# The last batch of a two-layer graph kernel: three side jobs moved earlier in the queues, and the last aggregation finished block by block

## The chip, the cores and the metric

The kernel runs on one core of a Trainium2 chip. The core has five engines with a queue each: TensorE (PE in the profile, with its weight loads as PEld), VectorE (DVE), ScalarE (ACT), GpSimd (POOL) and SyncE (SP), which here only issues DMAs. Each queue is worked off in the order in which the program emits its instructions, and an instruction at the head that waits for another engine holds up all that is queued behind it.

The metric is the time of one execution on the device, in microseconds, as the median of several runs. Before the change it is 2584.24 us, over three runs from 2582.49 to 2584.95 us.

## The reference

32 batches of 512 rows by 512 columns pass through two layers. Cut to what matters:

```
# layer 0: attention with 8 heads of 64, masked by adj, then a residual and a norm
q, k, v = x @ Wq + bq, x @ Wk + bk, x @ Wv + bv
scores  = q k^T / sqrt(64) + where(adj == 0, -1e9, 0)
x = layernorm(x + softmax(scores) v)
# layer 1: aggregation over the graph, a weight, a bias, a residual and a norm
y = adj @ x
x = layernorm(x + y @ weight + bias)
```

adj is a 512 by 512 matrix of zeros and ones, the same for all batches. The layer norm has no learned scale.

## The kernel before

A batch's rows are four blocks of 128 rows (the index c, r or row below), its columns four blocks of 128 columns (the index d). `X[b]` holds a batch's rows in SBUF. There is one tile for an even and one for an odd batch, and a separate one, `xlast`, for batch 31. The program is emitted in one long hand-made order: nothing reorders it, and it is this order that the change edits.

To keep float32 accuracy[...], the kernel splits each factor. For layer 1 the rows are split into a high half (ACT, `split` L503 or `split_rows` L537) and a low half (POOL, L504 or L538). **Aggregation** is y = adj @ x: eight matmuls for each block d of y, four with high halves and four with low halves. For batches 0 to 30 it is `aggregate` (L520), block by block: as soon as a block's eight matmuls are done, `split_y` (L514) splits it into three factors: high on ACT (`split_high`, L304), rest on DVE (`split_rest`, L307), both on POOL (`split_both`, L310). **Convolution** is y @ weight: `convolve` (L569) runs three passes of four matmuls for each row block into two PSUM banks, NEAR (high and rest factors) and FAR (both factors), so 48 matmuls for a batch and all eight banks. `add_row` (L578) then adds NEAR (L561) and FAR (L565) to `X[b]` on DVE, which also sets the banks free. The **bias** is added to `X[b]` on POOL (`add_bias`, L540). The **second norm** is: statistics of each row block on DVE (`statistics`, L477 and L478), one square root on ACT (L481), a reciprocal and four small products on DVE (`invert_root`, L486 and L488), one pass over each row block on ACT (`normalise`, L493); then `store` (L506) sends the batch out through SP. The tables for the norm are called by batch plus layer: `norm(t - 1, 1)` with t = 31 is batch 29's second norm, because layer 1 runs one batch behind, and `norm(t, 1)` is batch 30's. In the same way `norm(t, 0)` is batch 31's first norm.

In the main loop (`iteration`, L800) three batches are under way at once, and the side jobs of the older two are strewn among the matmuls of the youngest. The change leaves this loop alone. It edits what comes after it.

- `last_halves(31)` (L874): batch 31's attention; batch 29's last two row blocks are convolved and added; batch 30's rows are split (`splits`) and aggregated (`gathered`).
- The end (L959 on), with t = 31: batch 30 is convolved; batch 31's first norm, with `split_rows` after each normalised row block; batch 29's last statistics, second norm and store; batch 30's `add_row`s, last bias and statistics; batch 30's second norm; `aggregate_rows(31)` (L543); convolution of 31; `judge` (L713), five tiny DVE operations that say whether any value ran out of range; batch 30's store; and last, row block by row block, batch 31's adds, statistics, root, norm and store.

`aggregate_rows` has the row block c as its outer loop, so that it may begin when the first row block is normalised, and needs four banks at once. The banks are handed out in turn out of eight. Since the convolution of batch 30 just before took all eight, the aggregation waits until batch 30's first rows are added:

```
    run(survey(t - 2)[NB // 2:] + norm(t - 1, 1))
    store(t - 2)
    run([(add_row, t - 1, r) for r in range(NB)] + biases(t - 1)[3:] + survey(t - 1))
    run(biases(t)[:2] + norm(t, 1)[:2])
    aggregate_rows(t)
```

`survey(b)` is the four statistics of batch b, `biases(b)` its four bias additions, and `merge(a, b)` emits a[0], then all of b[0], then a[1], then all of b[1], and so on.

Of the kernel before, what the change touches and what calls it, by code (L numbers as in the profile page):

```python
# [18 lines left out]
P = 128  # L19
# [163 lines left out]
def fast_kernel(ctx: ExitStack, tc, verdict, x, adj, Wq, bq, Wk, bk, Wv, bv, W1, b1, out):  # L183
    nc = tc.nc
# [3 lines left out]
    NB = N // P  # L188
    DB = D // P
# [10 lines left out]
    def bank(*shape):  # L200

        return psum.tile([P, *shape], FP, name="bank", tag="bank", bufs=8)

    def plain(t):

        return t.bitcast(FP)
# [69 lines left out]
    adjT = work.tile([P, NB, N], FR, name="adjT", bufs=1)  # L276
# [26 lines left out]
    def split_high(high, a):  # L303
        nc.scalar.activation(high, a, AF.Copy, scale=EPSILON * SHRINK)  # L304

    def split_rest(rest, high, a):
        nc.vector.scalar_tensor_tensor(rest, plain(high), -1.0 / EPSILON, a, op0=ALU.mult, op1=ALU.add)  # L307

    def split_both(both, high, rest, engine=nc.gpsimd):
        engine.tensor_sub(both, plain(high), plain(rest))  # L310
# [16 lines left out]
    def factors():  # L327
        return [work.tile([P, DB, N], FR, name=f"factors{f}", bufs=1) for f in (HIGH, REST, BOTH)]
# [36 lines left out]
    def splits_of_x(b):  # L365
        return [[(f, b, d) for d in range(DB)] if b < B else [] for f in (high_of_x, rest_of_x, both_of_x)]
# [102 lines left out]
    STAT, RSTD, SHIFT, HIGHS, LOWS = {}, {}, {}, {}, {}  # L469
# [36 lines left out]
    def store(b, blocks=None):  # L506
        for c in blocks or ():
            nc.sync.dma_start(out[b, c * P:(c + 1) * P, :], X[b][:, c, :])
        if blocks is None:
            nc.sync.dma_start(out[b].rearrange("(c p) d -> p c d", p=P), X[b])  # L510

    YT = {}
# [27 lines left out]
    def add_bias(b, c):  # L540
        nc.gpsimd.tensor_add(X[b][:, c, :], X[b][:, c, :], b1_r)  # L541

    def aggregate_rows(b):  # L543

        banks = [bank(N) for _ in range(DB)]
        for c in range(NB):
            for d, pm in enumerate(banks):
                for part in (HIGHS[b, c], LOWS[b, c]):
                    nc.tensor.matmul(pm, part[:, d * P:(d + 1) * P], adjT[:, c, :],
                                     start=(c == 0 and part is HIGHS[b, c]), stop=(c == NB - 1 and part is LOWS[b, c]))  # L550
        YT[b] = factors()
        high, rest, both = ([YT[b][f][:, d, :] for d in range(DB)] for f in range(3))
        for d, pm in enumerate(banks):
            split_high(high[d], pm)
            split_rest(rest[d], high[d], pm)
        for d in range(DB):
            split_both(both[d], high[d], rest[d], nc.gpsimd if d < 2 else nc.vector)

    def add_near(b, r, near):
        row = X[b][:, r, :]  # L560
# [8 lines left out]
    def convolve(b, passes):  # L569

        yt = YT[b]
        for r, f, blocks in passes:
            if (b, r) not in NEAR:
                NEAR[b, r], FAR[b, r] = bank(N), bank(N)
            one_pass(f, (FAR if f == BOTH else NEAR)[b, r], lambda f, d: yt[f][:, d, r * P:(r + 1) * P],
                     lambda f, d: w1[:, f, d, :], blocks)
# [5 lines left out]
    def whole(r):  # L582
        return [(r, f, range(DB)) for f in (HIGH, REST, BOTH)]
# [5 lines left out]
    def aggregation(b):  # L589

        return [[(f, b, d) for d in range(DB)] if b >= 0 else [] for f in (split, aggregate)]
# [31 lines left out]
    def attend(b, hp):  # L623
        po = bank(N)
        for j in range(NB):
            e = E.pop((b, hp, j))
            for s in range(2):
                h = 2 * hp + s
                nc.tensor.matmul(po[s * HD:(s + 1) * HD, :], V[b, j][:, h * HD:(h + 1) * HD], e[:, s, :],  # L629
                                 start=(j == 0), stop=(j == NB - 1))  # L630
        OUT[b, hp] = po

    def turn_out(b, hp):

        po = OUT.pop((b, hp))
        at = AT[b, hp] = work.tile([P, N], FP, name="attT")
        if b == B - 1:
            nc.scalar.activation(at, po, AF.Copy)
            return

        nc.vector.transpose(at, po)  # L641
        TURNED[b, hp] = passing.tile([P, N], FP, name="turned")
        nc.sync.dma_start(TURNED[b, hp], at)
# [26 lines left out]
    def fetch_parts(b, g):  # L670

        part = PART[b, g].rearrange("p a c h -> p a (c h)")
        passed = PASSED.pop((b, g)).rearrange("(a r) i x -> i r a x", r=SQ)
        for i in range(P // SQ):
            nc.sync.dma_start(part[i * SQ:(i + 1) * SQ, :, :], passed[i])

    def add_up(b, g):

        both = work.tile([P, 2, NB, GROUP], FP, name="inverse")
        total, inverse = both[:, 0, :, :], both[:, 1, :, :]  # L680
        nc.vector.tensor_reduce(total, PART.pop((b, g)).rearrange("p a c h -> p c h a"), axis=AX.X, op=ALU.add)
        nc.vector.reciprocal(inverse, total)  # L682
        nc.gpsimd.tensor_add(watched, watched, both)
        INVERSE[b, g] = inverse
# [16 lines left out]
    def turn_back(b, hp):  # L701

        pt = OUT[b, hp] = bank(NB, 2, HD)
        for c in range(NB):
            nc.tensor.transpose(pt[:, c, :, :], AT[b, hp][:, c * P:(c + 1) * P], ident)
# [7 lines left out]
    def judge():  # L713
        seen = consts.tile([P, 3], FP, name="seen")
        nc.vector.tensor_reduce(seen[:, 0:2], watched.rearrange("p k c h -> p k (c h)"), axis=AX.X, op=ALU.add)
        nc.vector.tensor_reduce(seen[:, 2:3], inexact, axis=AX.X, op=ALU.add)
        well = consts.tile([P, 4], FP, name="well")
        nc.vector.tensor_scalar(well[:, 0:2], seen[:, 0:2], BOUND, None, op0=ALU.is_le)
        nc.vector.tensor_scalar(well[:, 2:3], seen[:, 2:3], 0.0, None, op0=ALU.is_equal)
        nc.vector.tensor_reduce(well[:, 3:4], well[:, 0:3], axis=AX.X, op=ALU.min)  # L720
        return well[:, 3:4]

    def run(units):
        for unit in units:
            unit[0](*unit[1:])
# [3 lines left out]
    pm = bank(P)  # L729
# [38 lines left out]
    def norm(t, which):  # L768

        if t - which < 0:  # L770
            return []
        lo, hi = which * NB, (which + 1) * NB
        return [(square_root, t, slice(lo, hi)), (invert_root, t, slice(lo, hi))] + [
            (normalise, t, slot) for slot in range(lo, hi)]

    def folds(b, g):
        return [(fold_squares, b, hp) for hp in range(g * PAIRS, (g + 1) * PAIRS)]

    def survey(b, which=1):

        return [(statistics, b, which, c) for c in range(NB)] if b >= 0 else []
# [5 lines left out]
    def biases(b):  # L787
        return [(add_bias, b, c) for c in range(NB)] if b >= 0 else []

    def merge(units, behind):  # L790

        merged = []
        for k in range(max(len(units), len(behind))):
            merged += units[k:k + 1] + (behind[k] if k < len(behind) else [])
        return merged

    def take_scores(b, g):
        run(scores(b, g))
# [75 lines left out]
    def last_halves(b):  # L874

        splits, gathered = aggregation(b - 1)
        young = norm(b - 1, 0)
        attend(b, 0)
        turn_out(b, 0)
        attend(b, 1)  # L880
        turn_out(b, 1)
        fetch_parts(b, 0)
        add_up(b, 0)
        take_scores(b, 1)
        turn_back(b, 0)
        turn_back(b, 1)
        run(young[:1] + [(last_residual, b, 0), (last_residual, b, 1)] + young[1:2] + folds(b, 1)[:1])
        for r in range(NB // 2, NB):
            convolve(b - 2, whole(r))
        run([(add_row, b - 2, r) for r in range(NB // 2, NB)] + young[2:] + splits)  # L890
        attend(b, 2)
        turn_out(b, 2)
        attend(b, 3)
        turn_out(b, 3)
        turn_back(b, 2)
        turn_back(b, 3)
        run(folds(b, 1)[1:] + [(pass_parts, b, 1), (fetch_parts, b, 1)])
        old, shift = biases(b - 2)[NB // 2:], biases(b - 1)
        run(merge(gathered, [old[:1], [], [(add_up, b, 1), (last_residual, b, 2)],
                             [(last_residual, b, 3)] + old[1:] + shift[:3]]))  # L900

    ends = project_first_two()
    for n in (2, 3):
# [46 lines left out]
    high, rest, both = splits_of_x(1)  # L950
# [8 lines left out]
    t = B - 1  # L959
# [3 lines left out]
    for c in range(NB):  # L963
        run(ahead[2 + c:3 + c])
        split_rows(t, c)
    run(survey(t - 2)[NB // 2:] + norm(t - 1, 1))
    store(t - 2)
    run([(add_row, t - 1, r) for r in range(NB)] + biases(t - 1)[3:] + survey(t - 1))
    run(biases(t)[:2] + norm(t, 1)[:2])
    aggregate_rows(t)  # L970
    convolve(t, FIRST_TWO + whole(2) + whole(3))
    run(biases(t)[2:] + norm(t, 1)[2:])
    well = judge()
    store(t - 1)
    pm = bank(N)
    nc.tensor.matmul(pm[0:1, 0:1], well, ones[:, 0:1], start=True, stop=True)
# [46 lines left out]
```

## Time and profile before

| | us |
|---|---|
| median of 3 runs | 2584.24 |
| the profiled execution, on the device | 2581.66 |
| its span, first to last instruction | 2579.7 |
| around the span | 1.96 |
| PE busy in the span | 2562.5 |
| DVE / POOL / ACT busy | 2062.6 / 1750.6 / 1527.1 |
| end of the main loop's last matmul of values, about | 2483.9 |
| last matmul of batch 31's convolution ends, about | 2570.5 |

The profile is one execution, so its times are positions on one line: 2550 means 2550 us after the first instruction. All that the change touches lies in the last 80 us, about 3% of the span. PE does matmuls with 512 columns at a steady pace there: the 24 of one convolution half take 5.44 us in the chain of waits, 0.227 us for one. A single matmul's duration in the trace is longer (about 0.39 us), since they are pipelined; the pace is what counts in sums.

### The profile page before, as it was taken

The numbers are of one execution on the slowest core, as the hardware profiler recorded it, in microseconds if no ns is written. First come the engines' busy times: TensorE is split into PE (matmuls) and PEld (weight loads), VectorE is DVE, ScalarE is ACT, GpSimd is POOL, SyncE is SP. The second block draws the span as 40 slices with busy tenths as digits, with TensorE's granted clock in tenths as the row PEclk, the third lists the DMA queues.
The fourth block names the chain that finished last, engine by engine and source line by source line (L and its number), as shares of the span: only waits on it lengthen the run. The fifth ranks groups of instructions, "written<-read, shape, count | busy, mean of one in ns | idle before, by whom it ended". The sixth has DMA issues, their size and how long they took to land.

```text
span 2579.7 us, 35703 instructions
## 1 busy us (share of the span) xinstructions
PE 2562.5 (99%) x11324; PEld 1695.0 (66%) x11324; DVE 2062.6 (80%) x3797; ACT 1527.1 (59%) x2540; POOL 1750.6 (68%) x1103
## 2 busy tenths in 40 slices
PE   9999999999999999999999999999999999999997
PEld 6676666766676666767666676666666676666665
DVE  8778878788787788877887878878788787788877
ACT  5656755656555666556565565655566655666554
POOL 4776677666676666766667666667666676676766
PEclk9999999999999999999999999999999999999999
DMA  9555554555545645446555455454554544645521
GB/s 267 165 157 145 164 155 112 168 147 158 166 105 156 177 131 159 127 139 173 139 158 141 121 168 146 156 162 102 162 161 149 161 118 144 178 136 153 141 80 51
DMA packets 675042, 380.47 MB, mean 147 GB/s; under 512 B 586912, under 2 KB 591264, under 8 KB 674848
## 3 DMA queue, kind: packets, MB, share of 16 engines
q1 hardware_dynamic: 674416, 377.48, 51.7%
q8 instruction: 92, 1.51, 0.2%
q14 instruction: 102, 0.84, 0.1%
q10 hardware_dynamic: 432, 0.66, 0.1%
HBM read 303.57 MB, written 74.45 MB: 147 GB/s over the span
## 4 chain that ended last, share of the span: by engine, by line
PE 97%; DVE 2%; ACT 0%; issue 0%; POOL 0%; DMA 0%; DVEq 0%; POOLq 0%; ACTq 0%
PE bank L417 53%; PE bank L606 18%; PE bank L629 17%; PE bank L526 9%; DVE e L608 0%; DVE bnst L477 0%; DMA xin<-in_x_dram 0%; POOL xs L541 0%; DVE factors L310 0%; DVE factors L307 0%; DVE xlast L561 0%; DVE xs L561 0%; PE bank L336 0%; DVE xlast L565 0%; ACT halves L537 0%
## 5 line engine op out<-in xcount | busy, mean ns | idle before, releaser
L610 ACT ACTIVATE e<-e 128x1024 f32<-128x1024 f32 x512 | 525.1, 1055 | 301.0 <-DVE e L608 262.4
L417 PE MATMUL bank<-factors,stream 128*128 128x512 f32 x3012 | 701.6, 392 | 0.8 <-DVE k L429 0.8
L417 PEld LDWEIGHTS bank<-factors,stream 128*128 128x128 f32 x3012 | 560.4, 188 | 162.7 <-DVE e L608 23.5
L621 POOL TENSOR_TENSOR es<-es,e 128x1024 f32<-128x1024 f32 x256 | 616.1, 2407 | 20.1
L608 DVE SCALAR_TENSOR_TENSOR e<-gap,bank 128x512 f32<-128x512 uint8 x1024 | 617.9, 681 | 12.1 <-PE bank L606 12.1
L621 POOL TENSOR_TENSOR es<-e 128x1024 f32<-128x1024 f32 x128 | 306.7, 2396 | 420.8 <-ACT e L610 420.8
L606 PE MATMUL bank<-q,k 64*128 64x512 f32 x2048 | 464.4, 598 | 0.0
L629 PE MATMUL bank<-e,v 128*64 128x512 f32 x2048 | 453.6, 595 | 0.0
L606 PEld LDWEIGHTS bank<-q,k 64*128 64x128 f32 x2048 | 204.2, 186 | 258.6 <-issue 164.0
L417 PE MATMUL bank<-w,factors 128*128 128x512 f32 x1536 | 354.8, 390 | 1.2 <-DVE factors L310 1.2
L417 PE MATMUL bank<-wv,factors 128*128 128x512 f32 x1536 | 353.5, 389 | 0.0
L310 POOL TENSOR_TENSOR factors<-factors,factors 128x512 fp32r<-128x512 f32 x253 | 320.1, 1286 | 35.4 <-DVE factors L307 30.8
L695 ACT ACTIVATE rows<-rows,zero,inverse 128x64 f32<-128x64 f32 x992 | 335.1, 429 | 8.8 <-DVE inverse L682 8.8
L417 PEld LDWEIGHTS bank<-w,factors 128*128 128x128 f32 x1536 | 288.0, 188 | 62.5 <-DVE factors L310 1.8
L417 PEld LDWEIGHTS bank<-wv,factors 128*128 128x128 f32 x1536 | 288.3, 188 | 60.5 <-DVE e L608 0.8
L629 PEld LDWEIGHTS bank<-e,v 128*64 128x64 f32 x2048 | 141.4, 137 | 278.4 <-issue 265.0
L503 ACT ACTIVATE high<-xs 128x512 fp32r<-128x512 f32 x124 | 74.4, 627 | 333.3 <-PE bank L526 333.2
L504 POOL TENSOR_TENSOR low<-xs,high 128x512 fp32r<-128x512 f32 x124 | 159.5, 1301 | 154.8 <-PE bank L526 154.8
L541 POOL TENSOR_TENSOR xs<-xs,b_r 128x512 f32<-128x512 f32 x124 | 159.7, 1289 | 130.6 <-DVE xs L565 130.6
L641 DVE STREAM_TRANSPOSE attT<-bank 128x512 f32<-128x512 f32 x124 | 87.7, 708 | 156.3 <-PE bank L629 156.3
L493 ACT ACTIVATE xs<-xs,shift,rstd 128x512 f32<-128x512 f32 x248 | 181.6, 806 | 15.2 <-DVE shift L488 15.2
L699 POOL TENSOR_TENSOR xs<-xs,rows 128x512 f32<-128x512 f32 x124 | 160.9, 1311 | 22.4 <-ACT rows L695 12.8
(98 smaller groups left out, 2441.6 us busy)
## 6 DMA issues: line engine op xcount, KB each, us to landing
stream<-kept_q SPq DMA_DIRECT2D x124, 768.0 KB, 6.0
stream<-kept_k SPq DMA_DIRECT2D x124, 768.0 KB, 4.5
xin<-in_x_dram SPq DMA_DIRECT2D x496, 64.0 KB, 2.5
turned<-attT SPq DMA_DIRECT2D x124, 256.0 KB, 3.2
rows<-turned SPq DMA_DIRECT2D x496, 64.0 KB, 2.6
xs<-in_x_dram SPq DMA_DIRECT2D x31, 1024.0 KB, 6.1
out_dram<-xs SPq DMA_DIRECT2D x31, 1024.0 KB, 5.2
part<-passed SPq DMA_DIRECT2D x256, 8.0 KB, 1.7
```

The lines of the kernel that those rows point to most:

```text
L310: engine.tensor_sub(both, plain(high), plain(rest))
L417: nc.tensor.matmul(pm, left(f, d), right(f, d), start=(f != REST and d == 0), stop=(f != HIGH and d == DB - 1))
L493: nc.scalar.activation(row, row, AF.Identity, bias=SHIFT[t][:, slot:slot + 1], scale=RSTD[t][:, slot:slot + 1])
L526: nc.tensor.matmul(pm, part, adjT[:, n % NB, :], start=(n == 0), stop=(n == 2 * NB - 1))
L541: nc.gpsimd.tensor_add(X[b][:, c, :], X[b][:, c, :], b1_r)
L606: nc.tensor.matmul(ps[s], keys[:, j * P:(j + 1) * P], queries, start=True, stop=True)
L608: nc.vector.scalar_tensor_tensor(e[:, s, :], gap[:, j, :], NEG * root, ps[s], op0=ALU.mult, op1=ALU.add)
L610: nc.scalar.activation(e, e, AF.Exp, scale=1.0 / root)
L621: nc.gpsimd.tensor_add(ES[b, hp], ES[b, hp] if j > 1 else E[b, hp, 0], E[b, hp, j])
L629: nc.tensor.matmul(po[s * HD:(s + 1) * HD, :], V[b, j][:, h * HD:(h + 1) * HD], e[:, s, :], start=(j == 0), stop=(j == NB - 1))
L695: nc.scalar.activation(part, part, AF.Identity, bias=zero, scale=inverse[:, c, s:s + 1])
L699: nc.gpsimd.tensor_add(cols, cols, ROWS.pop((b, hp)))
```

## The change

Five things are different, all after the main loop:

1. In `last_halves`, the bias for batch 29's row blocks 2 and 3 is no longer added in the middle of and after batch 30's aggregation. It is added between the first low halves of batch 30.
2. Batch 29's last two statistics come directly after batch 31's last fold of exponential sums. Its second norm is strewn over batch 30's aggregation: the square root behind block 0's split, the reciprocal and products behind block 1's, the four normalisations behind block 3's. Its store follows there. Batch 30's four biases all come behind it.
3. At the end, the row additions of batch 30 and its statistics therefore come straight after the first norm of batch 31 and its splits.
4. Batch 30's square root and reciprocal are no longer ahead of the last aggregation but amid it (`amid`), behind the splits of blocks 0 and 1. One bias addition of batch 31 is ahead of it and three are behind the convolution's emission, where two and two were before.
5. `aggregate_rows` takes row blocks 0 and 1 for all column blocks, then finishes each column block d with row blocks 2 and 3, and splits it with `split_y`. All four `split_both` are on POOL; before, blocks 2 and 3 were on DVE. `judge` is emitted before the last convolution instead of after it, in both cases behind the splits on DVE.

```diff
-    def aggregate_rows(b):
+    def aggregate_rows(b, amid):
 
         banks = [bank(N) for _ in range(DB)]
-        for c in range(NB):
-            for d, pm in enumerate(banks):
-                for part in (HIGHS[b, c], LOWS[b, c]):
-                    nc.tensor.matmul(pm, part[:, d * P:(d + 1) * P], adjT[:, c, :],
-                                     start=(c == 0 and part is HIGHS[b, c]), stop=(c == NB - 1 and part is LOWS[b, c]))
+        half = range(NB // 2), range(NB // 2, NB)
+        order = [(c, d) for c in half[0] for d in range(DB)] + [(c, d) for d in range(DB) for c in half[1]]
+        for c, d in order:
+            for part in (HIGHS[b, c], LOWS[b, c]):
+                nc.tensor.matmul(banks[d], part[:, d * P:(d + 1) * P], adjT[:, c, :],
+                                 start=(c == 0 and part is HIGHS[b, c]), stop=(c == NB - 1 and part is LOWS[b, c]))
         YT[b] = factors()
-        high, rest, both = ([YT[b][f][:, d, :] for d in range(DB)] for f in range(3))
-        for d, pm in enumerate(banks):
-            split_high(high[d], pm)
-            split_rest(rest[d], high[d], pm)
-        for d in range(DB):
-            split_both(both[d], high[d], rest[d], nc.gpsimd if d < 2 else nc.vector)
+        run(merge([(split_y, b, d, pm) for d, pm in enumerate(banks)], amid))
...
-        run([(add_row, b - 2, r) for r in range(NB // 2, NB)] + young[2:] + splits)
+        run([(add_row, b - 2, r) for r in range(NB // 2, NB)] + young[2:])
+        old, shift = biases(b - 2)[NB // 2:], biases(b - 1)
+        run(merge(splits, [old[:1], old[1:]]))
...
-        run(folds(b, 1)[1:] + [(pass_parts, b, 1), (fetch_parts, b, 1)])
-        old, shift = biases(b - 2)[NB // 2:], biases(b - 1)
-        run(merge(gathered, [old[:1], [], [(add_up, b, 1), (last_residual, b, 2)],
-                             [(last_residual, b, 3)] + old[1:] + shift[:3]]))
+        run(folds(b, 1)[1:] + [(pass_parts, b, 1), (fetch_parts, b, 1)] + survey(b - 2)[NB // 2:])
+        elder = norm(b - 1, 1)
+        run(merge(gathered, [elder[:1], elder[1:2], [(add_up, b, 1), (last_residual, b, 2)],
+                             [(last_residual, b, 3)] + elder[2:] + [(store, b - 2)] + shift]))
...
-    run(survey(t - 2)[NB // 2:] + norm(t - 1, 1))
-    store(t - 2)
-    run([(add_row, t - 1, r) for r in range(NB)] + biases(t - 1)[3:] + survey(t - 1))
-    run(biases(t)[:2] + norm(t, 1)[:2])
-    aggregate_rows(t)
+    run([(add_row, t - 1, r) for r in range(NB)] + survey(t - 1) + biases(t)[:1])
+    younger = norm(t, 1)
+    aggregate_rows(t, [younger[:1], younger[1:2]])
+    well = judge()
     convolve(t, FIRST_TWO + whole(2) + whole(3))
-    run(biases(t)[2:] + norm(t, 1)[2:])
-    well = judge()
+    run(biases(t)[1:] + younger[2:])
     store(t - 1)
```

## The prediction

> **What bounds the kernel now.** I read the page's chain of waits first, then PE's own timeline over the last 60 us, then the timelines of DVE, ACT and POOL at the places where PE stops, and last the clock by stages.
>
> From the page, the busy line and the chain by engine:
>
> ```profile
> PE 2562.5 (99%) x11324; PEld 1695.0 (66%) x11324; DVE 2062.6 (80%) x3797; ACT 1527.1 (59%) x2540; POOL 1750.6 (68%) x1103
> PE 97%; DVE 2%; ACT 0%; issue 0%; POOL 0%; DMA 0%; DVEq 0%; POOLq 0%; ACTq 0%
> ```
>
> PE sets the time; all its idle time together is 2579.7 - 2562.5 = 17.2 us. The edits remove no matmul, so they can win only idle time, a slow clock or the tail after PE's last matmul. PE's timeline shows where these lie (start, duration, line; in brackets the idle time before and what ended it):
>
> ```profile
> 2532.75 11.51 PE L417 MATMUL bank<-w,factors 128*128 128x512 f32 x48
> 2548.05 9.59 PE L549 MATMUL bank<-adjT,halves 128*128 128x512 f32 x32 [3.80 <-DVE xs L561]
> 2557.48 4.09 PE L417 MATMUL bank<-w,factors 128*128 128x512 f32 x15
> 2562.75 7.75 PE L417 MATMUL bank<-w,factors 128*128 128x512 f32 x33 [1.17 <-DVE factors L310]
> ```
>
> PE waits 3.80 us for DVE's L561 (batch 30's first row addition, which frees a bank), and 1.17 us for DVE's L310 (the factors "both" of blocks 2 and 3). The windows over PE (start:end, length, busy, clock, DMA share, GB/s) add a third loss:
>
> ```profile
> 2544.20:2548.00 3.80, 0.06 (x1) 1.00 0.01 2
> 2549.30:2552.50 3.20, 3.20 (x9) 0.53 0.50 195
> ```
>
> After the pause PE ran 3.2 us at half clock: its 32 aggregation matmuls took 2557.48 - 2548.05 = 9.43 us where 32 x 0.227 = 7.26 would do, so 2.2 us more. Now DVE, ACT and POOL there:
>
> ```profile
> 2540.28 0.58 DVE L488 TENSOR_SCALAR shift<-stat,rstd 128x1 f32<-128x1 f32 x4
> 2540.78 0.68 DVE L477 BATCH_NORM_STATS2 bnst<-xs 128x6 f32<-128x512 f32 x1
> 2546.52 0.18 DVE L486 RECIPROCAL rstd<-rstd 128x4 f32<-128x4 f32 x1 [4.04 <-ACT rstd L481]
> 2547.22 0.68 DVE L561 SCALAR_TENSOR_TENSOR xs<-bank,xs 128x512 f32<-128x512 f32 x1
> 2562.82 1.04 DVE L718 TENSOR_SCALAR well<-seen 128x2 f32<-128x2 f32 x1
> ```
>
> ```profile
> 2545.67 0.63 ACT L537 ACTIVATE halves<-xlast 128x512 fp32r<-128x512 f32 x1
> 2546.20 0.28 ACT L481 ACTIVATE rstd<-stat,eps 128x4 f32<-128x4 f32 x1
> ```
>
> ```profile
> 2522.92 5.01 POOL L504 TENSOR_TENSOR low<-xs,high 128x512 fp32r<-128x512 f32 x4
> 2536.38 5.03 POOL L541 TENSOR_TENSOR xs<-xs,b_r 128x512 f32<-128x512 f32 x4
> 2546.37 1.27 POOL L538 TENSOR_TENSOR halves<-xlast,halves 128x512 fp32r<-128x512 f32 x1 [0.15 <-ACT halves L537]
> 2560.42 3.42 POOL L541 TENSOR_TENSOR xlast<-xlast,b_r 128x512 f32<-128x512 f32 x2
> ```
>
> At 2542.3 DVE has nothing in the way of batch 30's additions except a reciprocal for batch 29. That waits 4.04 us for a square root, which ACT reaches only at 2546.20, behind batch 31's four normalisations and splits. The additions queue behind it, and PE behind them. So a job that nobody needs holds the critical path.
>
> [...] 3.80 idle, then 3.2 us near 0.5; the 1.17 us pause brought no drop. [...] L718 (two elements a partition) took 1.04 us and ended at 2563.86, with POOL's bias (2560.42 + 3.42 = 2563.84), while DVE's row additions (one PSUM, one SBUF input) kept 0.69 beside biases at 1.28.
>
> **Part by part.** *Biases of batch 29 amid the low halves (POOL).* Four L504 at 1.25 each ran from 2522.92. Two L541 of 1.25 go between: low 0 ends 2524.2, bias 2525.4, low 1 2526.7, bias 2527.9, low 2 2529.2, low 3 2530.4. PE takes the lows at 2526.39, 2528.22, 2530.03, 2531.84. All are in time, the tightest (low 2) by 0.8 us. The biases wait for DVE's additions of batch 29, over by 2523.0. POOL's "both" operations now start 2530.4: three end at 2534.2, the fourth waits as before for its rest (2535.0) and ends at 2536.4. One bias fewer afterwards, one more of batch 30: four L541 to 2541.4, as now. Cost nothing.
>
> *Batch 29's statistics and norm.* Row block 2's statistics run at 2525.5, row block 3's wait for the bias at 2527.9 and end at 2528.9; behind them on DVE stands rest 0 (before 2528.20), 0.7 late, whose reader on POOL isn't free before 2530.4. The square root on ACT, 2528.9 to 2529.2, stands before high 1, which PE lets start at 2529.3. Reciprocal and products (0.18 + 0.58) fit in DVE's idle 1.1 us before rest 2. No table load: the trace has none after 2516.75, with square roots and copies mixed. Normalisations (2.9 us) go into ACT's idle 6.2 us after 2533.5. The store of 1 MB is issued near 2536.5 instead of 2549.94; SP has only later stores behind it. Cost nothing up to 2540.86, where batch 31's first products end.
>
> *Additions of batch 30 straight after.* Eight operations took 2547.22 to 2552.80; they run 2540.8 to 2546.4. Their banks are full in time (PE ends row block 2 near 2541.1, row block 3 near 2543.9), their biases end at 2541.4. The first bank is free at 2541.5, long before PE is, so PE's next limit is its own end, 2544.1. The halves follow ACT and POOL: low 0 ends 2543.4, the others 2544.8, 2546.2, 2547.6. With row blocks 0 and 1 first (16 matmuls, to 2547.7) the last low is wanted at 2548.4: no pause, no half clock. Aggregation then ends at 2544.1 + 7.26 = 2551.35 instead of 2557.48: 3.95 + 2.2 = 6.1 us won.
>
> *Statistics of batch 30, splits of 31.* Four statistics took 3.2 us (2552.80 to 2556.0): now to 2549.6. PE finishes block 0 at 2548.75, high 0 ends 2549.4, so rest 0 waits for DVE: 2549.6 to 2550.2. The added wait on ACT: the square root (2549.6 to 2549.9) has high 1 to 3 behind it, which are wanted 2549.6, 2550.6, 2551.5; only high 1 is 0.3 late. DVE: rest 1 to 2551.2, norm to 2551.9, rests 2 and 3 to 2553.1, `judge` from 2553.1, about 1.4 us[...]. POOL: four "both" from 2550.25 at 1.25 to 1.30, to 2555.5[...]. Their price lies between 5.0 (no contention) and 6.8 (1.7 each, as the two L541 in the 3.42 row); I take 5.2[...].
>
> *Convolution of 31.* It starts 2551.35; "both 3" is wanted at its 16th matmul, 2551.35 + 15 x 0.227 = 2554.75, so PE still pauses about 0.7 us and resumes at 2555.5 instead of 2562.75: 7.25 won. The 33 matmuls left end near 2563.1.
>
> *The tail.* Before, `judge` made DVE late: its first far addition began at 2564.83, 2.1 us after PE resumed. Now `judge` is over at 2554.5 and FAR 0 is full at 2555.9, so the addition begins at 2555.95: 8.9 won. From there each row costs DVE 2.46 (2564.83 to 2572.26 over three rows), and PE's row blocks come at 2.72, the last at 2563.2: the last addition begins near 2563.4, with the verdict's tiny matmul before it (0 to 0.4). POOL's three later biases end at 2556.8, 2558.0, 2559.3, each about 0.7 us or more before DVE asks. From the last addition to the end stays 2579.7 - 2572.26 = 7.44.
>
> Sum: span 2563.4 + 7.44 = 2570.85, 8.85 less than 2579.7; about 2572.8 with the 1.96 around it. The profiled run (2581.66) lies 2.6 under the median, so I carry the difference over: 2584.24 - 8.85 = 2575.4.
>
> **The rivals.** *A, the above*, with 7.0 to 9.3 us won: 2574.9 to 2577.2.
> *B, POOL becomes the limit or a half-clock stretch stays.* If "both" costs 1.7 each, PE and the tail come 1.6 later (7.2 won); if PE is slowed once for 3.2 us, 2.2 (6.6 won). For: POOL is packed from 2542 to 2559. Against: the rows at 1.25 to 1.30. About 6.7 won: 2577.5; both together 5.0.
> *C, no change.* DVE's additions and POOL's low halves, apart until now, run side by side. [...] Against: the 0.69 beside 1.28 above.
> *D, slower.* The biases of batch 29 stand on POOL before low 1 and low 2, and wait for DVE. Cover is 0.8 us; each us beyond is PE idle, plus 2.2[...]. It is slower than before when they are late by 8.85 + 0.8 - 2.2 = 7.45 us; at 10 us late, 2584.24 + 10 - 0.8 + 2.2 - 8.85 = 2586.8. For: the wait is new. Against: what they wait for was over 1.2 us before their turn.
>
> **How the numbers follow.** A 0.75, B 0.13, C 0.08, D 0.04. The time is A's, 2575.4. The runs before spread over 2.5 us, so 1.3 goes on A's ends (2573.6 to 2578.5), and B draws the upper end out: 2573.0 to 2579.0. A measurement can tell about 0.2% (5.2 us) from no change. Faster by more than that: nearly all of A and three quarters of B, 0.82. Within it: C and the rest, 0.14. Slower: D, 0.04.
>
> **What would show it.** PE's timeline: no pause before the 32 aggregation matmuls, which take about 7.3 us at full clock; one pause below 1 us in the last convolution, ended by POOL's L310. DVE: the first batch 30 addition near 2540.8, directly after the products. POOL: L310 at 1.25 to 1.3. The span near 2571. Wrong would be a pause before a low half of batch 30 (D), additions of over 1 us (C), or a clock under 1 in the aggregation (B).

## The result, and the profile after

The changed kernel took 2576.52 us in the median of 8 runs (2574.0 to 2578.16); the kernel before took 2584.26 in 8 runs beside them (2582.41 to 2586.3). The ratio is 0.9969, with a 95% interval from 0.9960 to 0.9978: about 8.0 us less (5.7 to 10.3), 2576.5 where 2575.4 was predicted. The profiled execution of the changed kernel had a span of 2575.9 us, so against the profile of before the gain looks like 3.8 us only. That is a trap, and the first thing to clear up.

A profile is one execution, and executions differ by a few us before they reach the part that the change edits. A place that both have, and that the change doesn't touch, makes the ends comparable: the start of the first L526 matmul of batch 30's aggregation (PE's timeline, first before, then after):

```profile
2525.38 1.18 PE L526 MATMUL bank<-adjT,high 128*128 128x512 f32 x4
```

```profile
2530.50 1.18 PE L526 MATMUL bank<-adjT,high 128*128 128x512 f32 x4
```

From there to the end (the **end stretch** below) it is 2579.69 - 2525.38 = 54.3 us before and 2575.94 - 2530.50 = 45.4 us after. The end became 8.9 us shorter; this one execution lost 5.1 us earlier.

PE's timeline of the changed kernel (start, duration, then the idle time before in brackets):

```profile
2537.87 11.52 PE L417 MATMUL bank<-w,factors 128*128 128x512 f32 x48
2549.23 7.42 PE L550 MATMUL bank<-adjT,halves 128*128 128x512 f32 x32
2556.49 3.56 PE L417 MATMUL bank<-w,factors 128*128 128x512 f32 x15
2560.51 7.77 PE L417 MATMUL bank<-w,factors 128*128 128x512 f32 x33 [0.46 <-POOL factors L310]
2568.21 0.19 PE L972 MATMUL bank<-ones,well 128*1 128x1 f32 x2
```

The pause of 3.80 us is gone, and the 32 aggregation matmuls take 2556.49 - 2549.23 = 7.26 us instead of 9.43. In the last convolution 0.46 us of waiting is left of 1.17, for GpSimd's fourth "both" factor. VectorE's timeline shows the batch 30 additions (L557) directly behind batch 31's products (L488), and the first far addition (L561 at 2561.04) waiting for PE instead of for `judge`:

```profile
2545.41 0.57 DVE L488 TENSOR_SCALAR shift<-stat,rstd 128x1 f32<-128x1 f32 x4
2545.91 0.68 DVE L557 SCALAR_TENSOR_TENSOR xs<-bank,xs 128x512 f32<-128x512 f32 x1
...
2558.32 0.92 DVE L714 TENSOR_SCALAR well<-seen 128x2 f32<-128x2 f32 x1
...
2561.04 0.69 DVE L561 TENSOR_TENSOR xlast<-bank,xlast 128x512 f32<-128x512 f32 x1 [0.94 <-PE bank L417]
...
2568.51 0.67 DVE L561 TENSOR_TENSOR xlast<-bank,xlast 128x512 f32<-128x512 f32 x1
```

GpSimd's timeline has the four low halves of batch 31 (L538) beside those additions, still at 1.35 us each, and the four "both" factors in a row at 1.26:

```profile
2547.22 5.41 POOL L538 TENSOR_TENSOR halves<-xlast,halves 128x512 fp32r<-128x512 f32 x4 [0.69 <-ACT halves L537]
2552.59 1.30 POOL L541 TENSOR_TENSOR xlast<-xlast,b_r 128x512 f32<-128x512 f32 x1
2555.41 5.04 POOL L310 TENSOR_TENSOR factors<-factors,factors 128x512 fp32r<-128x512 f32 x4 [1.52 <-DVE factors L307]
```

What the account of the prediction did not use is the chain of waits in order of time. In the kernel before it reads, from 2546 us on:

```profile
2546.30 0.20 ACT rstd L481
2546.49 0.02 issue
2546.52 0.19 DVE rstd L486
...
2556.12 0.31 ACT rstd L481
...
2557.24 2.39 DVE factors L307 x4
2559.63 3.07 DVE factors L310 x2
2562.69 0.10 DVE seen L715
...
2562.86 1.01 DVE well L718
```

PE isn't in it any more: from ScalarE's square root at 2546.30 on, the chain is VectorE, broken only by ScalarE's next square root (batch 30's, at 2556.12) and by the root and normalisation of the very last row block. After the change it crosses GpSimd and PE:

```profile
2554.76 0.58 DVE factors L307
2555.34 0.07 issue
2555.41 5.05 POOL factors L310 x4
2560.46 0.04 issue
2560.51 0.51 PE bank L417
2561.02 0.02 issue
2561.04 0.70 DVE xlast L561
```

So there are two readings of the 8.9 us. **The PE account**, in which the prediction booked its gain: pause 3.95, slow clock 2.2, and so on. **The VectorE account**: additions 6.4 us earlier (their distance from the start of L488 falls from 2547.22 - 2540.28 = 6.94 us to 0.50), and 2.5 us between the first addition of batch 30 and the first far addition of batch 31 (17.61 before, 15.13 after). Both sums are near 8.9. The experiments separate them. The far addition before, from VectorE's timeline:

```profile
2564.83 0.69 DVE L565 TENSOR_TENSOR xlast<-bank,xlast 128x512 f32<-128x512 f32 x1
```

### The profile page after: what moved, and what is told of

It is laid out like the page before. It is cut to its first block, busy times and chain, and to the rows that moved or that the text cites. A ratio compares the mean times of both kernels' runs of the same rounds, so it can differ in the third digit from the quotient of the medians.

```text
span 2575.9 us, 35702 instructions
## 1 busy us (share of the span) xinstructions
PE 2562.7 (99%) x11324; PEld 1693.9 (66%) x11324; DVE 2058.9 (80%) x3795; ACT 1527.3 (59%) x2540; POOL 1751.0 (68%) x1105
## 4 chain that ended last, share of the span: by engine, by line
PE 94%; DVE 2%; DMA 1%; POOL 1%; ACT 1%; issue 0%; SPq 0%; DVEq 0%; ACTq 0%; POOLq 0%
PE bank L417 52%; PE bank L602 17%; PE bank L625 16%; PE bank L526 9%; DVE e L604 1%; DMA stream<-kept_k 0%; DMA turned<-attT 0%; DVE bnst L477 0%; DVE factors L307 0%; POOL es L617 0%; ACT e L606 0%; SPq L645 0%; POOL factors L310 0%; PE bank L729 0%; POOL wv L932 0%
## 5 line engine op out<-in xcount | busy, mean ns | idle before, releaser
L310 POOL TENSOR_TENSOR factors<-factors,factors 128x512 fp32r<-128x512 f32 x255 | 322.1, 1284 | 33.9 <-DVE factors L307 32.0
```

## The experiments

All times in the table are in us. "End stretch" is from the profile, "runs" is the ratio to the kernel before, measured beside it, with its 95% interval.

| kernel | end stretch | runs |
|---|---|---|
| before | 54.3 | |
| changed | 45.4 | 0.9969 (0.9960 to 0.9978) |
| x1, before with the pause filled | 54.3 | 0.9998 (0.9990 to 1.0007) |
| x2, before with edit 5 alone | 53.1 | 0.9996 (0.9987 to 1.0005) |
| x3, changed without edits 4 and 5 | 48.1 | 0.9973 (0.9962 to 0.9983) |
| x4, before with a swap | 52.8 | 0.9992 (0.9983 to 1.0001) |
| x5, before without batch 29's root, products and norm | 49.5 | 0.9983 (0.9975 to 0.9990) |
| x6, swap with both roots first | 49.9 | 0.9982 (0.9975 to 0.9989) |
| y1, changed, two "both" on VectorE | 46.8 | 0.9970 (0.9959 to 0.9981) |
| y2, changed without edit 4 | 46.6 | 0.9972 (0.9960 to 0.9983) |
| y3, changed, lows 2.7 us late | 47.8 | 0.9975 (0.9967 to 0.9984) |
| y4, changed, lows 8.1 us late | 54.2 | 0.9994 (0.9985 to 1.0003) |

An interval is about 2 us to each side, so the runs confirm the sizes and the profiles tell the small steps. Each kernel has one profile, and from the last far addition to the end, a stretch with the last store in it, the twelve take 7.40 to 7.78 us: a difference below 0.4 us in the second column says little by itself.

**x1: is the slow clock behind PE's pause worth anything?**

```diff
-    convolve(t - 1, FIRST_TWO + whole(2) + whole(3))
+    convolve(t - 1, FIRST_TWO + whole(2) + whole(3) + 4 * [(3, BOTH, range(DB))])
```

> The kernel before, with the last pass of batch 30's convolution (row block 3, factors both, four matmuls) done five times instead of once: 16 matmuls more, 16 x 0.227 = 3.6 us, which fill most of the pause before the last aggregation and leave the values as they were. If PE's pause and its half clock are on the path, as the prediction's terms 3.95 + 2.2 add them up: the aggregation's 32 matmuls take 7.3 us instead of 9.4, and the span from PE's first L526 of batch 30 to the end (54.3 us before) is about 2.2 us shorter. If VectorE's chain alone sets the end (square root of batch 29, eight additions, four statistics, square root, products, four rests): the aggregation is as fast, and the end doesn't move, within 0.2 us.

PE's timeline of x1:

```profile
2534.05 15.13 PE L417 MATMUL bank<-w,factors 128*128 128x512 f32 x64
2549.36 8.29 PE L549 MATMUL bank<-adjT,halves 128*128 128x512 f32 x32 [0.17 <-DVE xs L561]
2558.26 4.62 PE L417 MATMUL bank<-w,factors 128*128 128x512 f32 x15 [0.61 <-ACT factors L304]
2564.06 7.82 PE L417 MATMUL bank<-w,factors 128*128 128x512 f32 x33 [1.18 <-DVE factors L310]
```

The pause is down from 3.80 to 0.17 us, and the windows over the aggregation (length, PE busy, clock, DMA share, GB/s) show full clock:

```profile
2549.30:2551.50 2.20, 2.08 (x7) 1.00 0.00 0
2551.50:2553.50 2.00, 2.00 (x9) 1.00 0.64 251
2553.50:2557.60 4.10, 4.10 (x19) 1.00 0.38 137
```

The end stretch did not move (54.28 against 54.32). PE now waits 0.61 us behind the aggregation, for the split that stands behind batch 30's square root: what it did faster it waited for later. So the slow clock was worth nothing in the kernel before. About the pause itself x1 says less: filled or not, the aggregation begins 22.7 us behind the first L526 (2549.36 - 2526.68 in x1, 2548.05 - 2525.38 before), since it waits for the same addition. x4 below is the kernel that starts it earlier. A side result: at full clock the aggregation still took 8.29 us, 0.9 more than the 7.42 of the changed kernel. The weight loads of x1 waited (us in total, times, longest):

```profile
PEld bank L549 <- DVE xs L565: 0.9, 2, 0.5
PEld bank L549 <- ACT xs L493: 0.6, 1, 0.6
PEld bank L549 <- DVE xs L561: 0.3, 1, 0.3
```

Of these 1.8 us 1.2 ended with VectorE's additions, which free the banks. Of the 2.2 us that the prediction put down to the half clock, 9.59 - 8.29 = 1.3 were the clock, and 8.29 - 7.42 = 0.9 came with these waits.

**x2 and x3: block order or moved side jobs?** x2 is the kernel before with the new `aggregate_rows` and this at the end:

```diff
-    aggregate_rows(t)
+    aggregate_rows(t, [])
+    well = judge()
     convolve(t, FIRST_TWO + whole(2) + whole(3))
     run(biases(t)[2:] + norm(t, 1)[2:])
-    well = judge()
```

> The kernel before with edit 5 alone: the last aggregation finishes block by block, all four both factors on GpSimd, judge emitted before the convolution, nothing moved in last_halves, and batch 30's square root and products ahead of the aggregation. VectorE's chain theory: the pause and the half clock stay, the first rest begins as before (L488 of batch 30 ends 2557.2), GpSimd's four both end 5.1 us later near 2563.0, so PE resumes 0.25 us later than before, but judge no longer stands behind two slow L310: the first far addition comes 1.4 us earlier, and the stretch from the first L526 of batch 30 to the end is 54.3 - 1.4 = 52.9 us. If the block order is what the change lives on, it is 5 us or more.

x3 is the changed kernel with the old `aggregate_rows` and this, so that edits 1 to 3 are left:

```diff
-    run([(add_row, t - 1, r) for r in range(NB)] + survey(t - 1) + biases(t)[:1])
+    run([(add_row, t - 1, r) for r in range(NB)] + survey(t - 1) + biases(t)[:2])
     younger = norm(t, 1)
-    aggregate_rows(t, [younger[:1], younger[1:2]])
-    well = judge()
+    run(younger[:2])
+    aggregate_rows(t)
     convolve(t, FIRST_TWO + whole(2) + whole(3))
-    run(biases(t)[1:] + younger[2:])
+    run(biases(t)[2:] + younger[2:])
+    well = judge()
```

> The changed kernel without edit 5: side jobs moved as in the change, but the old aggregation by rows, batch 30's square root and products ahead of it, both factors of blocks 2 and 3 on VectorE, judge behind. VectorE's chain theory: additions start 0.5 us after batch 31's products, 6.4 us earlier than before; no pause, no half clock; then the old end with L310 on VectorE beside GpSimd's biases: 54.3 - 6.2 = 48.1 us from the first L526 of batch 30 to the end, that is 2.7 us longer than the change. If block order and moves are worth their parts independently: 54.3 - 8.9 + 1.4 = 46.8 us.

Measured: 53.1 for x2 (1.2 us won) and 48.1 for x3 (6.2 won). The moves carry the gain. 6.2 + 1.2 is 7.4, not 8.9, but edit 4 is in neither kernel: both keep batch 30's square root and products ahead of the aggregation. y2 below is x3 with edit 5 (and one bias addition placed later), at 46.6. So edit 5 is worth 1.2 us without the moves and 1.5 with them, and edit 4 the last 1.1. x2 also speaks on the clock: its aggregation took 10.23 us, 5.8 of them at half clock, longer than the 9.59 before, and its end stretch is still shorter.

**x4, x5 and x6: is the root of batch 29 the cause?** x4 only swaps the order at the end; `last_halves` stays as it was:

```diff
-    run(survey(t - 2)[NB // 2:] + norm(t - 1, 1))
-    store(t - 2)
+    run(survey(t - 2)[NB // 2:])
     run([(add_row, t - 1, r) for r in range(NB)] + biases(t - 1)[3:] + survey(t - 1))
+    run(norm(t - 1, 1))
+    store(t - 2)
```

> The kernel before with one swap at the end: batch 30's additions, bias and statistics are emitted before batch 29's square root, products, normalisation and store instead of behind them; last_halves and the aggregation as before. If the wait of VectorE for that square root is the cause: additions start near 2542.4 (behind the two statistics of batch 29) instead of 2547.2, 4.8 us earlier, but batch 30's statistic of row block 3 now waits for its bias (about 0.7) and batch 29's root and products (about 1.3) come behind it on the path: about 3 us won, 51.3 us from the first L526 of batch 30 to the end. If PE's wait was for something else, nothing is won.

Only 1.5 us were won, not 3. The additions did start early (17.0 us behind the first L526, against 21.8 before) and PE's pause was gone, but PE then stood still in another place, for the splits on ScalarE (PE's timeline):

```profile
2545.80 7.45 PE L549 MATMUL bank<-adjT,halves 128*128 128x512 f32 x32
2556.96 13.61 PE L417 MATMUL bank<-w,factors 128*128 128x512 f32 x48 [3.71 <-ACT factors L304]
```

ScalarE's timeline shows what was in the way: batch 29's four normalisations, which wait 5.09 us for products that VectorE now reaches only behind the additions and statistics, and batch 30's square root behind them:

```profile
2547.94 0.28 ACT L481 ACTIVATE rstd<-stat,eps 128x4 f32<-128x4 f32 x1
2553.31 2.93 ACT L493 ACTIVATE xs<-xs,shift,rstd 128x512 f32<-128x512 f32 x4 [5.09 <-DVE shift L488]
2556.14 0.28 ACT L481 ACTIVATE rstd<-stat,eps 128x4 f32<-128x4 f32 x1
2556.33 2.02 ACT L304 ACTIVATE factors<-bank 128x512 fp32r<-128x512 f32 x4
```

My expectation had priced VectorE's side of the swap and left out ScalarE's. This run also decides between the two accounts. The aggregation begins 18.7 us behind the first L526 (2545.80 - 2527.11), as in the changed kernel and 4.0 earlier than before, and runs at full pace, so it ends 6.1 us earlier than before. On the PE account that wins 6.1 us; it won 1.5, because the splits that PE needs next stand behind VectorE's and ScalarE's queues. The PE account falls.

Two more kernels test what the wait for the root is worth. x5 takes the root away, and all that follows from it:

```diff
-    run(survey(t - 2)[NB // 2:] + norm(t - 1, 1))
+    run(survey(t - 2)[NB // 2:])
     store(t - 2)
```

> The kernel before with batch 29's second norm left out behind its statistics (no square root, no products, no normalisation: batch 29 goes out without its last norm). All else keeps its place. If VectorE's chain sets the end and the wait for this root is its largest part: batch 30's additions start behind batch 29's statistics, 4.8 us earlier, nothing else on the chain changes, and the stretch from the first L526 of batch 30 to the end is 54.3 - 4.8 = 49.5 us. If PE's pause is what counts: PE then pauses nowhere before the aggregation and the gain is the pause and the slow clock, 3.8 + 1.1 or more: 49.4 at most as well, but PE would not wait for L304 behind the aggregation, as it must if VectorE is the limit.

x6 keeps the swap and sends the four normalisations behind the aggregation:

```diff
-    run(survey(t - 2)[NB // 2:] + norm(t - 1, 1))
-    store(t - 2)
+    run(survey(t - 2)[NB // 2:])
     run([(add_row, t - 1, r) for r in range(NB)] + biases(t - 1)[3:] + survey(t - 1))
+    run(norm(t - 1, 1)[:2])
     run(biases(t)[:2] + norm(t, 1)[:2])
     aggregate_rows(t)
+    run(norm(t - 1, 1)[2:])
+    store(t - 2)
```

> As x4_swap, but with batch 29's four normalisations and its store behind the last aggregation's splits, so that batch 30's square root no longer stands behind them on ScalarE. If those four (2.9 us on ScalarE, which wait for products that VectorE reaches only behind the additions and statistics) took back what the swap won: rest 0 begins 2.7 us earlier than in x4_swap, and the stretch is 52.8 - 2.7 = 50.1 us. If something else held x4_swap, it stays near 52.8.

x5 came to 49.45 us and x6 to 49.86. So the wait for that one square root, with the five small operations behind it on VectorE (4.04 us of waiting, about 0.7 of work), was worth 4.9 of the 8.9 us, and the normalisations took back 2.9 us in x4. In x5, too, PE has no pause before the aggregation and one of 0.61 us behind it, as x1 has; the expectation had named this as the sign that VectorE is the limit:

```profile
2547.69 7.41 PE L549 MATMUL bank<-adjT,halves 128*128 128x512 f32 x32
2555.72 4.61 PE L417 MATMUL bank<-w,factors 128*128 128x512 f32 x15 [0.61 <-ACT factors L304]
```

**y1 and y2: what are edits 4 and 5 worth?** In the changed kernel y1 undoes one part of edit 5 (`split_both` of blocks 2 and 3 goes back to VectorE), and y2, the second diff, undoes edit 4.

```diff
-        run(merge([(split_y, b, d, pm) for d, pm in enumerate(banks)], amid))
+        run(merge([(split_y, b, d, pm, nc.gpsimd if d < 2 else nc.vector) for d, pm in enumerate(banks)], amid))
```

> The changed kernel with the both factors of blocks 2 and 3 of the last aggregation on VectorE instead of GpSimd. [...] rest 3 and judge queue behind both 2: PE resumes about 0.7 us later than in the change, the first far addition 2.2 us later, and the stretch from the first L526 of batch 30 to the end is 45.4 + 2.2 = 47.6 us. If GpSimd's row of four (5.04 us) were the limit and VectorE had room: 0.5 us shorter than the change, 44.9.

```diff
-    aggregate_rows(t, [younger[:1], younger[1:2]])
+    run(younger[:2])
+    aggregate_rows(t, [])
```

> The changed kernel with batch 30's square root and products ahead of the last aggregation's splits instead of amid them. On ScalarE the root waits for the last statistic and holds up high 0; on VectorE the products come before rest 0: everything from the first both on is 1.2 us later, 46.6 us from the first L526 of batch 30 to the end. If PE has room for it (its last pause is 0.46 us, VectorE waits 0.94 us for the first far bank): 0.3 us or less.

y2 is 46.58: 1.1 us longer than the change, as expected. y1 is 46.76: 1.3 us longer, not 2.2. The expectation was an estimate with the two L310 at about their price in the kernel before (1.47 and 1.75 us there). On VectorE's timeline of y1 they were cheaper, and `judge`'s two-element operation was about as slow as in both kernels (1.04 us before, 0.92 in the change):

```profile
2555.54 0.88 DVE L310 TENSOR_TENSOR factors<-factors,factors 128x512 fp32r<-128x512 f32 x1
...
2557.05 1.07 DVE L310 TENSOR_TENSOR factors<-factors,factors 128x512 fp32r<-128x512 f32 x1
...
2558.25 1.05 DVE L714 TENSOR_SCALAR well<-seen 128x2 f32<-128x2 f32 x1
```

PE's part of y1 is even a little shorter (its last matmul starts 37.6 us behind the first L526, against 37.7), so the 1.3 us are VectorE's: two L310 and `judge` stand before the first addition of batch 31. The block order alone, without the move of the "both" factors, was not tried; if the parts add up, y1's 1.3 leave it 0.2 of edit 5's 1.5, less than one profile each can tell. Nor was edit 4 tried with the old order.

**y3 and y4: how far was the slower case?** Both compute the same low half several times, so that all four come later.

```diff
-        nc.gpsimd.tensor_sub(low, cols, plain(high))
+        for _ in range(3 if b == B - 2 and d == 0 else 1):
+            nc.gpsimd.tensor_sub(low, cols, plain(high))
```

> The changed kernel with the low half of block 0 of batch 30 computed three times instead of once (two more GpSimd operations of 1.25 us, the same values), so that all lows come 2.5 us later. Prediction's cover: low 2 had 0.8 us. Low 0 is 0.3 us late, low 2 1.7 us late: PE idles 1.7 us in the aggregation of batch 30, at full clock, and the stretch from its first L526 to the end is 45.4 + 1.7 = 47.1 us. If batch 30's aggregation is off the path, it stays at 45.4.

> The changed kernel with the low half of block 0 of batch 30 computed seven times (six more operations, 7.5 us late). Low 0 is then ready near 5.3 us after PE wants it[...]. The prediction's case D: PE idle 7.5 - 0.8 = 6.7 us and 2.2 us for the half clock behind the pause, in all 8.9: the stretch from the first L526 of batch 30 to the end is about 54.3 us, as long as before the change. If the half clock is hidden behind VectorE's chain: 52.1 us.

y3, with the repetition of the diff, is 47.8: 2.4 us longer than the change where 1.7 was expected; 0.3 of it lies in the last store. The idle times in PE's timeline make only 1.2:

```profile
2532.85 1.19 PE L527 MATMUL bank<-adjT,low 128*128 128x512 f32 x4 [0.43 <-POOL low L505]
2533.88 1.08 PE L527 MATMUL bank<-adjT,high 128*128 128x512 f32 x4
2535.35 1.20 PE L527 MATMUL bank<-adjT,low 128*128 128x512 f32 x4 [0.39 <-POOL low L505]
2536.38 1.07 PE L527 MATMUL bank<-adjT,high 128*128 128x512 f32 x4
2537.83 1.20 PE L527 MATMUL bank<-adjT,low 128*128 128x512 f32 x4 [0.38 <-POOL low L505]
```

Yet batch 30's convolution starts 9.44 us behind the first L526 instead of 7.37, 2.07 later: each wait costs about 0.69, not the 0.40 that the brackets show. The bracket counts from the modelled end of the group before, and that lies 0.17 us behind the point at which the next group starts at pace (groups are 1.08 long and 0.91 apart). So the group behind a wait starts 0.55 to 0.60 us later than without it, and the group after it loses 0.12 more. From 2531 to 2541 the clock is at 1.00.

y4 computes that low half seven times, and PE has one long pause; the windows over it (length, PE busy, clock, DMA share, GB/s):

```profile
2528.40:2534.20 5.80, 0.13 (x1) 0.85 0.08 10
2534.20:2539.40 5.20, 5.08 (x12) 0.51 0.00 0
2539.40:2543.10 3.70, 3.70 (x17) 1.00 0.00 0
```

The end stretch is 54.2 us: the whole gain is gone, where the prediction's slower case put its break-even at a delay of 7.45 us. That the totals meet is in part luck. The repeated operations took 1.34 us each, not 1.25 (low 0's first matmul starts 6.97 us behind the first L526, in y3 with four operations fewer 1.61), so the low halves came 8.1 us later. PE then starts on low 0 5.96 us later than in the changed kernel (6.97 us behind the first L526, against 1.01), not 6.7, because low 0 had 2.2 us of cover and not low 2's 0.8. And the slow clock cost more than 2.2: the 28 matmuls from 2534.32 to 2543.13 took 8.81 us instead of 28 x 0.227 = 6.36, 2.5 more. Here, in front of a chain without slack, the half clock does cost. The last 0.35 lies in the last store.

How long the half clock lasted was not the same everywhere. Before the change (pause 3.80 us) the clock stood at 0.50 for 3.41 us, from 1.5 us after PE had resumed. In x2 (pause 3.83 us) its mean from 2550.0, where PE resumed, to 2560.0 was 0.71: 5.8 us of PE's work at half clock, if only 0.50 and 1.00 are in the mean. In y4 (5.79) the means above, 0.85 and 0.51, make about 6.8 us at half clock in the same way, from about 1.9 us before PE resumed, 5.0 of them in PE's work. In x4 (3.71) the 48 matmuls behind the pause took 13.61 us, where batch 30's 48 took 11.48; x4's mean clock over the whole execution was 0.998, as before the change and in x2 and y4, and 0.999 in all other kernels. Pauses of nearly the same length (3.80 and 3.83) had different sequels; the runs don't show what decides.

## Why the prediction was right, and where its account was not

The prediction walked the engines from one milestone to the next. Counted from the first L526 of batch 30, so that the early part doesn't matter (2525.38 is taken off the predicted times, 2530.50 off the measured ones):

| milestone | predicted | measured |
|---|---|---|
| first addition of batch 30 | 15.4 | 15.4 |
| last aggregation starts | 18.7 | 18.7 |
| last convolution starts | 26.0 | 26.0 |
| PE resumes for "both 3" | 30.1 | 30.0 |
| first far addition of batch 31 | 30.6 | 30.5 |
| last far addition | 38.0 | 38.0 |
| end | 45.5 | 45.4 |

Point by point:

- *Biases, statistics and norm of batch 29 at no cost.* Right: batch 31's products end where they did relative to the first L526, and PE has no wait in batch 30's aggregation. The cover of low 2 was put at 0.8 us, and y3's trace bears it out. Low 2 ends 6.53 us behind the first L526 there and 3.81 in the changed kernel, 2.72 later rather than 2.5, and its group of matmuls starts 1.94 later, so 0.8 was free. The group after it loses the last 0.13 of the 2.07.
- *Additions straight after, at the old pace beside GpSimd.* Right, and case C is out: additions at 0.68 to 0.69 beside L538 at 1.35.
- *"6.1 us won" as 3.95 pause and 2.2 clock.* The aggregation did end 6.1 us earlier, but that is not where the gain comes from. x1 removes the slow clock and wins nothing; x4 ends the aggregation 6.1 us earlier and wins 1.5. The right terms are on VectorE: 6.4 by the earlier additions, of which the wait for batch 29's root is 4.9 by x5. The prediction had named this root as what holds VectorE, and PE behind it; its sums then booked the gain on PE. Also 2.2 was two things, 1.3 of clock and 0.9 of waits for the banks. The sum came out because the walk asked at every step for the latest of all engines.
- *Four "both" in 5.2 us, a pause of 0.7.* 5.04 and 0.46. The 5.2 was an estimate, from single GpSimd operations of 1.25 to 1.30 us.
- *The tail.* As worked out; `judge` lies in a gap of VectorE now.
- *A span near 2571.* Missed: 2575.9. The early part of this execution was 5.1 us longer: matched matmul by matmul, PE is 3.4 us behind the profile of before at the 2000th of its 11324 matmuls, near 457 us, and loses the rest slowly after that, in stages where both kernels have the same instructions. Over the 12 profiles the first L526 of batch 30 lies between 2525.4 and 2531.2 us, and the profile of before, from which the prediction read its 2525.4, is the earliest of all. Carrying the difference over to the median, not the span, was the sound step. In the first 500 us the changed kernel's PE waited 2.3 us for chunks of weights from DRAM, x3's 2.5, y4's 0.6, that of before not at all for these. These waits are not the whole of it, since x3 reached the first L526 only 2.1 us later than before. What differs from run to run stays open.

No version here beats the changed kernel. From the first L526 to its last matmul PE takes 37.7 us there, with one bracketed pause of 0.46; its 160 matmuls at 0.227 us would take 36.3. So, as an estimate from this pace, a better order of the same work could win at most 1.4 us before the last 7.7 us, which are one row block's additions, statistics, norm and store.

## What to carry to other kernels

Take the end of a kernel as a stretch from a common instruction, not as the difference of two spans. A pause of the busiest engine is a loss only if the chain of waits runs through it: follow the chain in order of time before booking the pause. Filling the pause with harmless work, as x1 does, tests only what the idleness brings with it, here the slow clock, since the next work starts no earlier. To test the pause itself, let its end come earlier and leave the rest of the chain as it was, as x4 nearly does. When a job is moved out of the way on one engine, look at once at what it leaves on the next engine's queue: the swap of x4 lost 2.9 of the 4.5 us that x6 wins to four operations that nobody needed yet.

## What the runs showed of the hardware

- The bracketed idle time before a group of matmuls understates a wait: three waits of about 0.40 us cost 0.69 each (y3).
- Behind a PE pause of 3.80 us (before) the clock was 0.50 for 3.41 us; behind 3.83 (x2) and 5.79 (y4) PE worked 5.8 and 5.0 us at half clock. Behind 3.71 (x4) 48 matmuls took 13.61 us instead of 11.48. Behind pauses of 1.17 (before) and 1.19 (x6) the clock was 1.00. In the end stretches no pause between batch 30's first L526 and PE's last matmul of values lies between 1.19 and 3.71 us, so from what length on the clock falls is not shown.
- The two L310 on VectorE before took 1.47 and 1.75 us, and ended 0.55 and 0.54 us after the GpSimd operation that was under way when they started. The two in y1 took 0.88 and 1.07 us; the first ended 0.55 us after such an operation.
